# qkv channels of the first pass as seven products of halves, with the sums on VectorE, and reciprocals of softmax sums on 16 columns

## The chip, the core and the metric

The kernel runs on one core of one Trainium2 chip. The metric is the device time in microseconds of one execution; the kernel before takes 4035.16 us (median of 3 runs, 4035.09 to 4043.93).

## The reference

Two layers act on 8 images x of 256 channels and 64 x 64 pixels, all in fp32. The change touches two places: the division by the softmax sums in the first layer, and the product that makes the qkv channels in the second.

```python
# layer 0: attention of all pixels to 16 x 16 reduced ones
xr = norm(conv(x, w_sr, stride 4))
q, (k, v) = w_q @ x, split(w_kv @ xr)
out = softmax(q k^T * d**-0.5) v          # 8 heads of 32
x = x + gamma_s * (w_out @ out)
# layer 1: linear attention on qkv and on a convolved copy of it
qkv = w_qkv @ x                           # 768 channels from 256
agg = grouped_1x1(depthwise_5x5(qkv))
att = relu_linear_attention(concat(qkv, agg))
x = x + batch_norm(w_proj @ att)
```

## The kernel before

Three passes follow one another. `first_pass` (L575) does layer 0 and the qkv channels and leaves the results in HBM; `second_pass` (L961) does the convolution and the key-value sums; `third_pass` (L1281) applies them. The change lies in the first pass alone.

An image is kept in SBUF as two blocks of 128 channels by 4096 pixels, and cut into 8 strips of 512 pixels (QB). Two neighbouring strips make one class of pixels (`cls`). The 768 qkv channels are six blocks of 128: j = 0, 1 are q, 2, 3 are k, 4, 5 are v. Blocks of q and k go to HBM as planes with a zero border (`stage`), blocks of k and v also as transposed tokens (`turned`).

The loop over n (L905) walks through 256 steps: image b, strip s, channel half c, key half kc. A step issues, in this order: four score tiles of four heads on 32 rows each (`scores`, L758) and their exponentials on ScalarE (L764); the product with the values for the step before (`valued`, L775); in every second step the sums over keys (`counted`, L791), which use exponentials added up by GpSimd (`joined`, L786), then the division (`normed`), and the next queries (L743). What remains of a strip is spread over four further steps: in the first the output projection and its addition to x (`added`, L809 and L810), then three times two of its six qkv blocks (`qkv`, L834). In the last steps of an image TensorE also makes the reduced keys and values of the next one (`keys_values`, L671 to L734), with a norm on VectorE (L687 to L713). During the first image VectorE multiplies out the weights of the convolution as well (L647), one piece a step.

A qkv block is two matmuls of 128 x 128 by 512 into one PSUM bank, one for each half of the input channels. Score tiles, queries, outputs and qkv blocks all come from one set of five banks:

```python
def bank(name):
    return psum.tile([P, 512], F32, tag="mm", name=name, bufs=5)
```

`qkv` lets ScalarE copy the bank into `stage` (L843) and VectorE transpose it into `turned` (L853). `normed` copies the product with the values out of PSUM on ScalarE (L798), takes the reciprocal of 512 columns on VectorE (L799) and multiplies (L800). The sums are the same on all 32 rows of a head, since `ones_w` has 32 equal columns. Within an engine, instructions run in the order in which the program was built, where a scheduler has moved some of them a little.

Of the kernel before, what the change touches and what calls it, by code (L numbers as in the profile page):

```python
# [27 lines left out]
F32 = mybir.dt.float32  # L28
AF = mybir.ActivationFunctionType
ALU = mybir.AluOpType  # L30
AX = mybir.AxisListType

P = 128
# [4 lines left out]
NB = HH // R  # L38
# [3 lines left out]
D0 = C // HEADS  # L42
D1 = 8
NH = P // D1
KS = 5
QB = 512
NG = HW // QB
# [527 lines left out]
def first_pass(ctx: ExitStack, tc: tile.TileContext, a, fine, planes, x2d, kd, vd, wtd):  # L575
    nc = tc.nc
    B = a.x.shape[0]
# [5 lines left out]
    two = ctx.enter_context(tc.tile_pool(name="two", bufs=2))  # L583
    made = ctx.enter_context(tc.tile_pool(name="made", bufs=1))
    rest = ctx.enter_context(tc.tile_pool(name="rest", bufs=2))

    psum_early = ctx.enter_context(tc.tile_pool(name="psum_early", bufs=1, space=bass.MemoryType.PSUM))
    psum = ctx.enter_context(tc.tile_pool(name="psum", bufs=1, space=bass.MemoryType.PSUM))

    def bank(name):  # L590
        return psum.tile([P, 512], F32, tag="mm", name=name, bufs=5)

    def load(src, name):
        consts[name] = const.tile(list(src.shape), F32, tag=name, name=name)
        nc.sync.dma_start(consts[name], src)

    consts, x_tiles = {}, {}
# [11 lines left out]
    def load_consts():  # L609
        for n, src in (  # L610
            ("wq", a.w_q), ("wkv", a.w_kv), ("vec", a.vecs), ("gam", a.gamma_s), ("wout", a.w_out),
            ("wqkv", a.w_qkv), ("wsmall", a.w_small),
        ):
            load(src, n)

    ident = const.tile([P, P], F32, tag="ident", name="ident")
    make_identity(nc, ident)
# [122 lines left out]
    def queries(b, s, c):  # L740
        ps = bank(f"q_{b}_{s}_{c}")
        for ci in range(2):
            nc.tensor.matmul(  # L743
                ps,
                consts["wq"][:, ci, c * P : (c + 1) * P],
                x_tiles[b][:, ci, s * QB : (s + 1) * QB],
                start=(ci == 0),
                stop=(ci == 1),
            )
        qs = two.tile([P, QB], F32, tag="q", name=f"q_{b}_{s}_{c}")  # L750
        nc.scalar.copy(qs, ps)
        return qs
# [12 lines left out]
            es.append(e)  # L765
        return es

    sums, flats, stages = {}, {}, {}

    def valued(b, s, c, kc, es):  # L770
        if kc == 0:
# [16 lines left out]
    def counted(b, s, c, es):  # L788
        sums["den"] = psum_early.tile([P, QB], F32, tag="den", name=f"den_{b}_{s}_{c}")
        for h in range(4):  # L790
            nc.tensor.matmul(sums["den"][h * D0 : (h + 1) * D0], ones_w, es[h], start=True, stop=True)  # L791

    def normed(b, s, c):
        av, den = sums["av"], sums["den"]
        i = 2 * ((b * NG + s) * 2 + c)
        att = rest.tile([P, QB], F32, tag="att", name=f"att_{b}_{s}_{c}", bufs=4)
        r = rest.tile([P, QB], F32, tag="rden", name=f"rden_{b}_{s}_{c}")
        nc.scalar.copy(att, av)  # L798
        nc.vector.reciprocal(r, den)  # L799
        nc.vector.tensor_mul(att, att, r)  # L800
        nc.scalar.activation(den, den, AF.Copy, accum_out=seen[:, i : i + 1])
        nc.scalar.activation(den, r, AF.Copy, accum_out=seen[:, i + 1 : i + 2])
        return att

    def added(b, s, att, oc):
        xt, cols = x_tiles[b], slice(s * QB, (s + 1) * QB)
        ps = bank(f"o_{b}_{s}_{oc}")
        for c in range(2):
            nc.tensor.matmul(ps, consts["wout"][:, c, oc * P : (oc + 1) * P], att[c], start=(c == 0), stop=(c == 1))  # L809
        nc.vector.scalar_tensor_tensor(  # L810
            xt[:, oc, cols], ps, consts["gam"][:, 0:1], xt[:, oc, cols], ALU.mult, ALU.add
        )
        nc.sync.dma_start(x2d[b][oc * P : (oc + 1) * P, cols], xt[:, oc, cols])


    def new_stage(b, s):
        st = rest.tile([P, 4, 2, NB + 1, NB + 1], F32, tag="stage", name=f"stage_{b}_{s}")
        row, col = (0 if s // 4 else NB), (0 if s // 2 % 2 else NB)
        v = st.rearrange("p j f y x -> p (j f) y x")
        nc.gpsimd.memset(v[:, :, row], 0.0)  # L820
        nc.gpsimd.memset(v[:, :, :, col], 0.0)
        return st

    def interior(st, s):
        y, x = s // 4, s // 2 % 2
        return st[:, :, :, y : y + NB, x : x + NB]


    turned = {}

    def qkv(b, s, st, j):
        ps = bank(f"qkv_{b}_{s}_{j}")
        for ci in range(2):
            nc.tensor.matmul(  # L834
                ps,
                consts["wqkv"][:, ci, j * P : (j + 1) * P],
                x_tiles[b][:, ci, s * QB : (s + 1) * QB],
                start=(ci == 0),
                stop=(ci == 1),
            )  # L840
        cls, al = s // 2, s % 2
        if j < 4:
            nc.scalar.copy(interior(st, s)[:, j], ps.rearrange("p (f y x) -> p f y x", f=2, y=NB))  # L843
            nc.sync.dma_start(
                planes[b, j].rearrange("g (k i l f) e -> g k i l (f e)", k=4, i=D1, l=2)[:, cls, :, al],
                st[:, j].rearrange("p f y x -> p (f y x)"),
            )
        if j < 2:
            return
        if al == 0:  # L850
            turned[j] = rest.tile([P, NB // 2, 4, D0], F32, tag=f"turned{j}", name=f"turned_{b}_{s}_{j}", bufs=1)
        t = turned[j]
        nc.vector.transpose(  # L853
            t[:, :, 2 * al : 2 * al + 2].rearrange("p y f e -> p f y e"),
            ps.rearrange("p (f y e) -> p f y e", f=2, y=NB // 2),
        )
        if al == 1:
            for k in range(4):
                n, src = 4 * (j % 2) + k, t[k * D0 : (k + 1) * D0].rearrange("p y f e -> p y (f e)")
                if j < 4:  # L860
                    dst = kd[b][n].rearrange("a (y w) x b e -> a b (w x) y e", w=2)
                    nc.sync.dma_start(dst[cls // 2, cls % 2], src)
                else:
                    dst = vd[b][n][1 : NB2 + 1, 1 : NB2 + 1]
                    dst = dst.rearrange("(y w a) (x b) e -> a b w x y e", w=2, a=2, b=2)
                    for w in range(2):
                        nc.sync.dma_start(dst[cls // 2, cls % 2, w], src[w * NB : (w + 1) * NB])

# [9 lines left out]
    first = queries(0, 0, 0)  # L880
# [1 line left out]
        pass  # L882
    load_x(1)
    order = [(b, s, c, kc) for b in range(B) for s in range(NG) for c in range(2) for kc in range(2)]
    q, es, att, fill = {0: first}, {}, {}, []
    ahead = iter(())


    def after(b, s):
        def make_out(oc):  # L890
            return lambda: added(b, s, [att[b, s, 0], att[b, s, 1]], oc)

        def make_qkv(j):
            def go():
                if j == 2:
                    stages[b, s] = new_stage(b, s)
                qkv(b, s, stages[b, s], j)

            return go

        q = [make_qkv(j) for j in range(6)]
        return [[make_out(0), make_out(1)], [q[2], q[4]], [q[3], q[5]], [q[0], q[1]]]

    n_all = len(order)
    for n in range(n_all + 6):  # L905
        m = n - 1
        if n < n_all:
            b, s, c, kc = order[n]
            es[n] = scores(b, s, c, kc, q[n // 2])
        if 0 <= m < n_all:  # L910
            valued(*order[m], es[m])
            if order[m][3] == 1:
                counted(*order[m][:3], es.pop(m - 1))
                es.pop(m)
                att[order[m][:3]] = normed(*order[m][:3])
        if n < n_all and kc == 1:
            joined(es[n - 1], es[n])
        if n < n_all and kc == 0 and n + 2 < n_all:
            q.pop(n // 2 - 1, None)
            q[n // 2 + 1] = queries(*order[n + 2][:3])  # L920
        if n >= 6 and (n - 6) % 4 == 0 and (n - 6) // 4 < B * NG:
            fill += after((n - 6) // 4 // NG, (n - 6) // 4 % NG)
        next(weights, None)
        if n < n_all:
            b, at = n // 32, n % 32
            if at == 2:
                border(b)
            if b + 1 < B:
                if at == 10 and b > 0:
                    load_x(b + 1)  # L930
                if at == 12:
                    ahead = keys_values(b + 1)
                if 12 <= at < 20:
                    next(ahead)
                    next(ahead)
                elif at >= 20:
                    next(ahead, None)
        if fill:
            for f in fill.pop(0):
                f()  # L940
    for _ in weights:
        pass

# [685 lines left out]
```

## Time and profile before

| stretch | what runs | us |
|---|---|---|
| 0 to 53 | loads and the first reduced keys | 53 |
| 53 to 345 | first image (32 steps) | 293 |
| 345 to 2104 | images 2 to 8 | 1759 |
| 2104 to 2134 | rest of the last two strips | 30 |
| 2134 to 4032 | second and third pass | 1898 |

In the page each engine has its busy time and share of the span. A group of instructions has its line, engine and operation, the tiles it writes and reads, how many there are, busy time in us and the mean duration of one in ns, then the idle time of the engine before them and who ended it. In a timeline a row has the start, the duration, the engine, the line and, behind x, how many like instructions are merged in it; a matmul of fp32 makes two records. In the first pass one step takes 5.7 to 8.3 us where no reduced keys are made beside it.

### The profile page before, as it was taken

Reading aid. Unit: us, or ns where it says so; the run is one execution under the profiler, and the core shown is the slowest. Engines: PE = TensorE matmul, PEld = TensorE weight load, DVE = VectorE, ACT = ScalarE, POOL = GpSimd, SP = SyncE. Lnnn points to the kernel's source line nnn. Section 1 sums busy time; section 2 is a strip of 40 time slices with the busy share of each in tenths; the row PEclk is TensorE's granted clock in tenths of the full one; section 3 lists DMA queues with packets and bytes.
Section 4 is the critical chain, followed back from the end, with each engine's and each line's share of the span. In section 5 each row is a group of like instructions: output and inputs, shape, how many; then the busy total and the mean of one; then the engine's idle time right before and its main releaser. Section 6 shows DMA issues by size and latency. Waiting matters only on the chain. (4 is left out here: it accounts for less than half of the span.)

```text
span 4031.7 us, 69469 instructions
## 1 busy us (share of the span) xinstructions
PE 3967.1 (98%) x27266; PEld 2322.3 (58%) x27266; DVE 1943.0 (48%) x2724; ACT 1666.0 (41%) x3505; POOL 1207.0 (30%) x1234
## 2 busy tenths in 40 slices
PE   8999999999999999999999999999999998999998
PEld 4433433434334344343337888888888886565565
DVE  2554344343443434434444566666666664444443
ACT  2345455454554544545552222222222223454454
POOL 2333233332333333323333344444444440000000
PEclk9999999999999999999999999999999999999999
DMA  7655435344444344443539888778778756767674
GB/s 236 205 178 155 128 92 146 103 105 144 104 136 115 95 143 105 132 115 92 145 102 253 240 227 236 219 220 237 218 220 237 202 168 172 234 197 235 199 231 138
DMA packets 588321, 691.32 MB, mean 171 GB/s; under 512 B 62160, under 2 KB 431312, under 8 KB 583760
## 3 DMA queue, kind: packets, MB, share of 16 engines
q1 hardware_dynamic: 587984, 686.79, 59.7%
q8 instruction: 216, 3.54, 0.4%
q14 instruction: 121, 0.99, 0.1%
HBM read 412.54 MB, written 274.10 MB: 170 GB/s over the span
## 5 line engine op out<-in xcount | busy, mean ns | idle before, releaser
L786 POOL TENSOR_TENSOR e<-e,e 128x512 f32<-128x512 f32 x512 | 651.9, 1307 | 1204.1 <-PE av L775 1190.2
L799 DVE RECIPROCAL rden<-den 128x512 f32<-128x512 f32 x128 | 429.7, 3357 | 688.0 <-PE den L791 688.0
L764 ACT ACTIVATE e<-sc 128x512 f32<-128x512 f32 x1024 | 529.3, 602 | 419.2 <-PE sc L758 419.2
L834 PE MATMUL qkv<-x,wqkv 128*128 128x512 f32 x1536 | 701.1, 599 | 0.0
L834 PEld LDWEIGHTS qkv<-x,wqkv 128*128 128x128 f32 x1536 | 285.3, 190 | 372.7 <-issue 354.0
L1085 PE MATMUL cv<-w,c 128*128 128x128 f32 x3072 | 386.9, 280 | 4.9 <-POOL c L1029 4.9
L1085 PEld LDWEIGHTS cv<-w,c 128*128 128x128 f32 x3072 | 360.9, 193 | 33.5 <-issue 27.0
L853 DVE STREAM_TRANSPOSE turned<-qkv 128x512 f32<-128x512 f32 x256 | 177.3, 707 | 338.8 <-ACT stage L843 282.0
L758 PE MATMUL sc<-q,kk 32*128 32x512 f32 x2048 | 324.2, 640 | 11.0 <-DVE x L810 7.3
L1127 PE MATMUL sums<-vq,r 128*32 128x288 f32 x4096 | 303.1, 410 | 0.0
L1452 DVE TENSOR_TENSOR y<-z,xs 128x256 f32<-128x256 f32 x256 | 142.6, 644 | 315.9 <-ACT z L1443 290.9
L1101 ACT ACTIVATE r<-s 128x512 f32<-128x512 f32 x256 | 160.5, 627 | 299.9 <-DVE s L1100 299.5
L843 ACT COPY stage<-qkv 128x512 f32<-128x512 f32 x256 | 150.1, 586 | 304.3 <-PE qkv L834 294.6
L775 PE MATMUL av<-e,vv 128*32 128x512 f32 x2048 | 274.3, 608 | 0.0
L1443 ACT ACTIVATE z<-p,bn 128x256 f32<-128x256 f32 x256 | 133.7, 578 | 314.5 <-PE p L1434 240.6
L1089 PE MATMUL cv<-c,w 128*128 128x128 f32 x2048 | 256.4, 279 | 0.0
L743 PE MATMUL q<-x,wq 128*128 128x512 f32 x512 | 253.8, 618 | 0.0
L1434 PE MATMUL p<-att,wproj 128*128 128x512 f32 x512 | 249.4, 609 | 2.2 <-ACT att L1417 2.2
L1092 ACT COPY both<-cv 128x512 f32<-128x512 f32 x128 | 75.0, 586 | 421.8 <-PE cv L1085 364.8
L1434 PE MATMUL p<-agg,wproj 128*128 128x512 f32 x512 | 242.3, 596 | 0.0
L1089 PEld LDWEIGHTS cv<-c,w 128*128 128x128 f32 x2048 | 242.2, 194 | 0.0
L671 PE MATMUL sr<-x,wsr 128*128 128x256 f32 x1024 | 234.6, 385 | 7.1 <-DMA wsr<-in_w_sr_dram 7.1
(121 smaller groups left out, 5107.8 us busy)
## 6 DMA issues: line engine op xcount, KB each, us to landing
vq<-v SPq DMA_DIRECT2D x256, 384.0 KB
planes<-stage SPq DMA_DIRECT2D x256, 289.0 KB
d<-planes SPq DMA_DIRECT2D x128, 578.0 KB
raw<-planes SPq DMA_DIRECT2D x128, 272.0 KB
x<-in_xp_dram SPq DMA_DIRECT2D x64, 512.0 KB
wsr<-in_w_sr_dram SPq DMA_DIRECT2D x128, 256.0 KB
x<-x SPq DMA_DIRECT2D x128, 256.0 KB
k<-turned SPq DMA_DIRECT2D x256, 128.0 KB
```

What stands on the lines that cost most here:

```text
L671: nc.tensor.matmul(ps[:, oc], w[:, ci, oc * P : (oc + 1) * P], xt[:, ci, f * NK : (f + 1) * NK], start=(f == ci == oc == 0), stop=(f == R ...
L743: nc.tensor.matmul(ps, consts["wq"][:, ci, c * P : (c + 1) * P], x_tiles[b][:, ci, s * QB : (s + 1) * QB], start=(ci == 0), stop=(ci == 1),)
L758: nc.tensor.matmul(scs[h], kks[b][rows, c, kc * P : (kc + 1) * P], qs[rows], start=True, stop=True)
L764: nc.scalar.activation(e, scs[h], AF.Exp, scale=D0**-0.5)
L775: nc.tensor.matmul(sums["av"][cols], vvs[b][:, kc, c * P + h * D0 : c * P + (h + 1) * D0], es[h], start=(kc == 0), stop=(kc == 1),)
L786: nc.gpsimd.tensor_tensor(es0[h], es0[h], es1[h], ALU.add)
L799: nc.vector.reciprocal(r, den)
L834: nc.tensor.matmul(ps, consts["wqkv"][:, ci, j * P : (j + 1) * P], x_tiles[b][:, ci, s * QB : (s + 1) * QB], start=(ci == 0), stop=(ci == 1),)
L1085: nc.tensor.matmul(out, x, m, start=(da == 0), stop=(da == 1))
L1089: nc.tensor.matmul(out, m, x, start=(da == 0), stop=(da == 1))
L1127: nc.tensor.matmul(ps[h * D0 : (h + 1) * D0, : 36 * D1].rearrange("p (r n e) -> p r n e", r=3, e=D1), kt[:, par, h, 2 * r + c], vq[:, r : ...
L1434: nc.tensor.matmul(ps.rearrange("p (f q n) -> p f q n", f=4, q=4), wproj[:, j, oc * P : (oc + 1) * P], src, start=(j == 0), stop=(j == 3),)
```

## The change

The two blocks of a pair (q, k or v) and two strips are taken together: two halves of output channels, two halves of input channels, two strips. This is a product of 2 x 2 blocks, and it is made by seven products instead of eight. The combinations of weights are made once (`combine_weights`), the differences of x once for two strips (three on VectorE, one on GpSimd), and the products are summed as they leave PSUM: each of the seven is a matmul that fills a bank alone, p1 is copied by ScalarE, and VectorE adds the others to partial sums in SBUF. p5 is read twice. The q blocks are summed straight into `stage`; k and v blocks go through a tile `whole`, from which VectorE transposes and, for k, ScalarE copies. The work of two strips is laid over eight steps, with 4, 3, 4, 0, 3, 4, 3 products behind a step with outputs and differences.

In `normed` the sums are transposed in blocks of 32 x 32, the reciprocal is taken on 16 columns, and a second transpose spreads it again. The aim is one matmul in eight less on TensorE, and less work in the reciprocal.

```diff
+    halves = ctx.enter_context(tc.tile_pool(name="halves", bufs=1))
...
+        combine_weights()
...
+        nc.vector.tensor_add(s1, a21, a22)
+        nc.vector.tensor_sub(s2, s1, a11)
+        nc.vector.tensor_sub(s3, a11, a21)
+        nc.vector.tensor_sub(s4, a12, s2)
...
-        r = rest.tile([P, QB], F32, tag="rden", name=f"rden_{b}_{s}_{c}")
+        r = rest.tile([P, NB, D0], F32, tag="rden", name=f"rden_{b}_{s}_{c}", bufs=1)
+        one = two.tile([P, NB], F32, tag="one", name=f"one_{b}_{s}_{c}")
         nc.scalar.copy(att, av)
-        nc.vector.reciprocal(r, den)
+        nc.vector.transpose(r.rearrange("p n d -> p (n d)"), den)
+        nc.vector.reciprocal(one, r[:, :, 0])
+        r = rest.tile([P, NB, D0], F32, tag="rall", name=f"rall_{b}_{s}_{c}", bufs=1)
+        nc.vector.transpose(r, one.unsqueeze(2).to_broadcast([P, NB, D0]))
+        r = r.rearrange("p n d -> p (n d)")
         nc.vector.tensor_mul(att, att, r)
...
+    def differences(b, g):
...
+        nc.vector.tensor_sub(t1, b12, b11)
+        nc.vector.tensor_sub(t2, b22, t1)
+        nc.gpsimd.tensor_tensor(t3, b22, b12, ALU.subtract)
+        nc.vector.tensor_sub(t4, t2, b21)
...
-        for ci in range(2):
-            nc.tensor.matmul(
-                ps,
-                consts["wqkv"][:, ci, j * P : (j + 1) * P],
-                x_tiles[b][:, ci, s * QB : (s + 1) * QB],
-                start=(ci == 0),
-                stop=(ci == 1),
...
+        def product(i, w, x):
+            ps = bank(f"qkv_{name}_{i}")
+            nc.tensor.matmul(ps, w, x, start=True, stop=True)
+            return ps
...
+        def ended(r, h, u, ps, op=ALU.add):
...
+            if not turned:
+                nc.vector.tensor_tensor(inside, rows(u), rows(ps), op)
+                return
+            whole = part("whole", 2)
+            nc.vector.tensor_tensor(whole, u, ps, op)
+            if stages:
+                nc.scalar.copy(inside, rows(whole))
+            nc.vector.transpose(
+                turned[r][:, :, 2 * h : 2 * h + 2].rearrange("p y f e -> p f y e"),
+                whole.rearrange("p (f y e) -> p f y e", f=2, y=NB // 2),
             )
...
+        def p1():
+            ps = product(1, w[:, 0, 0], b11)
+            u[1] = part(1)
+            nc.scalar.copy(u[1], ps)
+
+        def p2():
+            ended(0, 0, u[1], product(2, w[:, 1, 0], b21))
+
+        def p6():
+            u[2] = part(2)
+            nc.vector.tensor_add(u[2], u[1], product(6, s2, t2))
+
+        def p7():
+            u[3] = part(3)
+            nc.vector.tensor_add(u[3], u[2], product(7, s3, t3))
+
+        def p4():
+            ended(1, 0, u[3], product(4, w[:, 1, 1], t4), ALU.subtract)
+
+        def p5():
+            ps = product(5, s1, t1)
+            ended(1, 1, u[3], ps)
+            u[4] = part(4)
+            nc.vector.tensor_add(u[4], u[2], ps)
+            stored(1)
+
+        def p3():
+            ended(0, 1, u[4], product(3, s4, b22))
+            stored(0)
...
+            work = [outputs(b, s) + [lambda b=b, s=s: differences(b, s // 2)]]
+            products = [p for pair in (1, 2, 0) for p in qkv_lazy(b, s // 2, pair)]
+            for i in (4, 3, 4, 0, 3, 4, 3):
+                work.append(products[:i])
+                products = products[i:]
```

In the changed kernel's lines the sum of p6 is L932, that of p7 L936, the second sum of p5 (u[4]) L945, and the sums of `ended` L888 and L891.

## The prediction

> **What bounds the kernel now.** I read the page's busy times first, then the busy times of stretches (the first pass ends at 2134 us), then the timelines of TensorE and VectorE for one strip, and last the places where TensorE waits. In the page, and in the stretch 1000 to 2000 us, TensorE is the engine that is never idle:
>
> ```profile
> PE 3967.1 (98%) x27266; PEld 2322.3 (58%) x27266; DVE 1943.0 (48%) x2724; ACT 1666.0 (41%) x3505; POOL 1207.0 (30%) x1234
> ...
> L799 DVE RECIPROCAL rden<-den 128x512 f32<-128x512 f32 x128 | 429.7, 3357 | 688.0 <-PE den L791 688.0
> ...
> L834 PE MATMUL qkv<-x,wqkv 128*128 128x512 f32 x1536 | 701.1, 599 | 0.0
> ```
> ```profile
> 1000.00:2000.00 1000.00, 1000.00 (x4320) 411.20 (x4319) 409.88 (x348) 492.55 (x1030) 334.89 (x319) 1.00 0.43 119
> ```
> The columns of the second view are the stretch, its length, then the busy us of PE, PEld, DVE, ACT and POOL. VectorE works 41% of it, so shortening the reciprocal (3.36 us) frees an engine that nobody waits for; what counts there is latency. A full busy figure doesn't say that TensorE never waits, because overlapping matmul records cover gaps. The timeline shows that (start, us, what):
>
> ```profile
> 1908.13 1.14 PE L758 MATMUL sc<-q,kk 32*128 32x512 f32 x8
> 1909.20 1.07 PE L775 MATMUL av<-e,vv 128*32 128x512 f32 x8
> 1910.19 3.70 PE L834 MATMUL qkv<-x,wqkv 128*128 128x512 f32 x8
> 1913.83 1.14 PE L758 MATMUL sc<-q,kk 32*128 32x512 f32 x8
> ...
> 1918.57 3.60 PE L834 MATMUL qkv<-x,wqkv 128*128 128x512 f32 x8
> 1922.10 1.41 PE L758 MATMUL sc<-q,kk 32*128 32x512 f32 x8
> 1923.44 1.07 PE L775 MATMUL av<-e,vv 128*32 128x512 f32 x8
> ...
> 1928.06 1.14 PE L758 MATMUL sc<-q,kk 32*128 32x512 f32 x8
> ```
> A record lasts 599 ns but the next begins before it ends, so the spacing counts. Eight qkv records take 3.53 us (1918.57 to 1922.10): 8 x 0.43, and 0.09 for going over to the small score tiles. After an av group the first record costs 0.11 more (1910.19 to 1913.83). The steps of one strip last 8.27, 5.70, 8.27 and 5.97 us, from one score group to the next: 28.21 a strip, 56.42 for two. The 5.97 holds a wait of 0.27: the group at 1922.10 takes 1.34 until av where it takes 1.07 elsewhere. The next view shows what such a wait is:
>
> ```profile
> 1046.03 2.73 DVE L713 TENSOR_SCALAR xr<-xr,vec 128x256 f32<-128x256 f32 x2
> ...
> 1048.69 1.30 DVE L853 STREAM_TRANSPOSE turned<-qkv 128x512 f32<-128x512 f32 x2
> 1048.69 1.87 PE L758 MATMUL sc<-q,kk 32*128 32x512 f32 x8
> ...
> 1050.49 1.07 PE L775 MATMUL av<-e,vv 128*32 128x512 f32 x8
> ```
> Four score tiles and the qkv tiles share five PSUM banks. The fourth score tile takes a bank that VectorE has yet to read; VectorE was held by the norm, and the score group grew from 1.07 to 1.80 us. TensorE lost those 0.73 us for good.
>
> **What the Trainium skill says.** "TensorE: Matmul & The Clock Gate", Step-by-step: only weight loads are pulled ahead, matmuls stay in program order; so a score tile that waits holds all behind it, as the last view shows. "PSUM — Partial Sum Buffer", The four PSUM rules: a matmul output is at most one bank of 512 fp32; each product is thus a bank of its own, against two matmuls to a bank before. "SBUF — State Buffer", Who interferes with whom: a VectorE operation with both inputs in SBUF shuts out GpSimd's reads and is shut out by them, for whole instructions. The trace agrees: the square of xr (L689) took 1.29 us at 1030.84 beside GpSimd's additions and 0.69 at 41.32 without them.
>
> **The change, part by part.** *Removed on TensorE:* 96 groups (8 images, 4 pairs of strips, 3 pairs of channel blocks) go from eight matmuls to seven: 96 matmuls of two records, 192 x 0.43 = 82 us. In the built order two strips are again eight steps: outputs; 4 products; 3; 4; outputs; 3; 4; 3. Without waits they last 8.27 + 5.70 + 7.41 + 5.70 + 8.27 + 4.84 + 8.27 + 4.84 = 53.30 us, so 3.12 less than before (2.58 of work, 0.54 of old waits).
>
> *Added on VectorE:* seven sums a group instead of copies on ScalarE. For their durations the trace has three neighbours of the same form (a sum with one PSUM input, a transpose of its result, another such sum):
>
> ```profile
> 2301.11 0.69 DVE L1206 TENSOR_TENSOR tok<-ng,den 128x512 f32<-128x512 f32 x1
> 2301.84 0.71 DVE L1213 STREAM_TRANSPOSE att<-tok 128x512 f32<-128x512 f32 x1
> 2302.47 0.65 DVE L1100 TENSOR_TENSOR s<-cv,both 128x512 f32<-128x512 f32 x1
> ```
> So 0.73 from a sum to the transpose that needs it, 0.64 on to the next, 0.65 for a sum that follows another. VectorE starts 0.63 after the last record of a bank starts (1913.83 - 0.52 = 1913.31, to the transpose at 1913.93 in VectorE's timeline), and TensorE 0.05 after VectorE ends (in the view before, the first transpose ends at 1048.69 + 0.70 = 1049.39, and the fourth score tile starts 1.05 ahead of av, at 1049.44). By sums, two strips cost VectorE 21 x 0.65 + 8 x 0.7 + 3 differences of 0.7, against 4 x (3.36 - 0.71 - 0.25 - 0.71) saved on reciprocals (0.25 is interpolated between 3.36 for 512 columns and 0.55 for 64): about 9 us more in 57, under 60% busy. Throughput is no limit.
>
> *The new wait:* in the built program the fourth score tile after a step of products takes the bank of p6 (steps of 4) or p5 (steps of 3), in 172 of 192 steps. p5's bank is free only after both of its sums. With t = 0 at the first record of the step:
> - Step of 3, k channels: p4's sum starts at 0.43 + 0.63 = 1.06, its transpose 1.79, p5's first sum 2.43, u4 3.07, over at 3.72, TensorE 3.77. It would have come at 6 x 0.43 + 0.11 = 2.69. Wait 1.08.
> - The same for v channels, after av: all 0.11 later, wait 1.08.
> - Step of 3, q channels (no transposes): p5's first sum 1.39 + 0.63 = 2.02, u4 2.67, over 3.32, TensorE 3.37 against 2.80: 0.57.
> - Step of 4, k and v: p2's sum 2.02, transpose 2.75, p6's sum 3.39, over 4.04, TensorE 4.09 against 3.65: 0.44 each. For q, none: p6's sum is over at 3.47, as TensorE comes at 3.55.
>
> The sum is 1.08 + 1.08 + 0.57 + 0.44 + 0.44 = 3.61 for two strips. Behind a waiting score tile stand its av, den and all later matmuls, and no other engine's slack gives that back. Two strips: 53.30 + 3.61 - 56.42 = +0.5 us; times 31 (the last pair is the tail), +15.
>
> *Smaller terms (my estimates):* the differences contend with GpSimd (0.69 to 1.29, with the p2 sum behind them): 0.2 x 31 = 6. In the first image 32 multiplications for the weights (L647, 1952 ns mean) stand in VectorE's queue, some between p2's sum and its transpose or between p4 and p5; some five delay TensorE by about 2 us, 0 to 30 for the range: +10. In 7 steps with the norm the fourth score tile waits for the first one's exponential, about 1.8, where before it was 0.73: +2. Tail: 21 products of 0.86 = 18 us run beside 29 VectorE operations of 0.64 = 18.6, so a start and an end show: +1. The combinations of weights stand ahead of the first norm (first VectorE work at 40.53) and wait for wqkv, issued at 32.0: 0 to 3, taken as 1. Fewer and larger stores, fewer stage copies and the shorter reciprocal cost nothing on the path: their queues have idle time. Tiles of the later passes keep their addresses.
>
> Sum: 15 + 6 + 10 + 2 + 1 + 1 = +35, so 4035 + 35 = 4070.
>
> **Rivals.** (1) *The waits are hidden*, if the bank is free in time: then 3.12 x 32 = 100 us go, about 3940, or part of it. For it: VectorE has idle time over all. Against it: the wait is latency from p4 to u4, in an order that idle time can't change. 0.16. (2) *Break-even*: the waits sum to 3.1 instead of 3.6 and the first image costs little: within 12 us of 4035. 0.17. (3) *Longer chains*: a sum of the form takes 0.75, as the scalar_tensor_tensor at L810 does, which adds 0.3 to each of four chains (1.2 x 31 = +37), and the weights' multiplications cost 30 instead of 10: 4127 or more. 0.10. (GpSimd sets a floor under rival 1: its four additions, 4.94 us from 2.26 us after an odd score group at 1908.13, gate den 7.2 us after that group; a step of 3 comes there at 4.84 + 1.94 = 6.8, so some 0.4 would be lost in any case, twice a pair.)
>
> **How the numbers follow.** The forecast above has 0.57: 4047 to about 4120. Slower 0.57 + 0.10, within 0.3% 0.17, faster 0.16. The range 4012 to 4120 leaves out most of rival 1 and the far half of rival 3, 2 in 10.
>
> **What would show it.** Right: the score groups after products take about 2.1 us in steps of 3 and 1.5 in steps of 4, waiting for the sums of L932 and L945; two strips last near 57 us; qkv matmuls 1344 records. Wrong: score groups back at 1.07 and two strips at 53 to 54 us (rival 1); sums above 0.7 us (rival 3); or den waiting for GpSimd in place of the banks.

## The result and the profile after

The changed kernel takes 4055.15 us (median; 4052.98 to 4062.72), beside it the kernel before took 4034.73: ratio 1.0051, 95% interval 1.0038 to 1.0064. The change makes the kernel 20 us slower.

The page's first line and the stretch of 1000 to 2000 us of the kernel after (columns as before: stretch, length, busy us of PE, PEld, DVE, ACT, POOL, clock, DMA share, GB/s):

```profile
PE 3982.1 (98%) x27074; PEld 2318.8 (57%) x27074; DVE 2262.4 (56%) x3752; ACT 1644.2 (41%) x3473; POOL 1275.1 (31%) x1394
```
```profile
1000.00:2000.00 1000.00, 995.73 (x4166) 405.10 (x4165) 555.56 (x836) 475.99 (x998) 363.60 (x390) 1.00 0.45 117
```

192 matmul records are gone, and TensorE's busy time has still grown, from 3967.1 to 3982.1 us. VectorE works 56% of the stretch instead of 41%, so it isn't full. TensorE's timeline of a step of four products, one of three and their score groups shows where the matmul time went:

```profile
1922.34 1.88 PE L875 MATMUL qkv<-differences,combined 128*128 128x512 f32 x4
1924.14 1.64 PE L774 MATMUL sc<-q,kk 32*128 32x512 f32 x8
1925.72 1.06 PE L791 MATMUL av<-e,vv 128*32 128x512 f32 x8
...
1931.11 1.02 PE L875 MATMUL qkv<-x,combined 128*128 128x512 f32 x2
1932.06 2.17 PE L774 MATMUL sc<-q,kk 32*128 32x512 f32 x8
1934.16 1.07 PE L791 MATMUL av<-e,vv 128*32 128x512 f32 x8
```

A score group took 1.07 us until av. It takes 1.58 here after four products (1924.14 to 1925.72) and 2.10 after three (1932.06 to 1934.16): waits of 0.5 and 1.03. They count as busy, because the records on both sides of a wait overlap; that is how "busy" grew while work went. What the fourth score tile of the group at 1932.06 waits for is in VectorE's timeline:

```profile
1930.45 0.69 DVE L891 TENSOR_TENSOR part_whole<-part,qkv 128x512 f32<-128x512 f32 x1
1931.17 0.71 DVE L894 STREAM_TRANSPOSE turned<-part_whole 128x512 f32<-128x512 f32 x1
1931.81 0.65 DVE L891 TENSOR_TENSOR part_whole<-part,qkv 128x512 f32<-128x512 f32 x1
1932.38 0.68 DVE L945 TENSOR_TENSOR part<-part,qkv 128x512 f32<-128x512 f32 x1
```

These are p4's sum, its transpose, and both sums of p5, the last over at 1932.38 + 0.68 = 1933.06. Then p5's bank is free, and the fourth score tile starts 1.05 ahead of av, at 1934.16 - 1.05 = 1933.11. It is no single case: in images 2 to 8 the fourth score tile waits for VectorE and starts 1.05 us after the first in 49 groups, 0.52 in 48 and 0.59 in 28.

The eight steps of two plain strips (strips beside which no reduced keys are made; the other pairs are called pairs with keys) now last 8.77, 4.84, 9.30, 4.84, 8.84, 5.70, 7.92 and 6.73 us: 56.94, against 56.42 before. From the starts of the score groups, the first pass adds up so:

| stretch | before | after | difference |
|---|---|---|---|
| first image (32 steps) | 276.7 | 264.1 | -12.6 |
| images 2 to 7 | 1555.9 | 1578.9 | +23.0 |
| last image, to its last score group | 218.2 | 221.2 | +3.0 |
| from there to the end of the first pass | 29.5 | 38.1 | +8.6 |

With a start 0.5 earlier that is +21.4 (from unrounded times); the later passes add 1.3, together the 22.7 us between the two profiled spans. The products come later in the order than before, so part of the first image's gain is only work moved to the end.

### The profile page after: what moved, and what is told of

It reads as the page before. It is cut to its first block, busy times and chain, and to the rows that moved or that the text cites. A ratio compares the mean times of both kernels' runs of the same rounds, so it can differ in the third digit from the quotient of the medians.

```text
span 4054.4 us, 70276 instructions
## 1 busy us (share of the span) xinstructions
PE 3982.1 (98%) x27074; PEld 2318.8 (57%) x27074; DVE 2262.4 (56%) x3752; ACT 1644.2 (41%) x3473; POOL 1275.1 (31%) x1394
## 3 DMA queue, kind: packets, MB, share of 16 engines
q14 instruction: 131, 1.07, 0.1%
## 5 line engine op out<-in xcount | busy, mean ns | idle before, releaser
L774 PE MATMUL sc<-q,kk 32*128 32x512 f32 x2048 | 418.2, 641 | 7.5 <-ACT e L780 3.6
L891 DVE TENSOR_TENSOR part_whole<-part,qkv 128x512 f32<-128x512 f32 x256 | 170.7, 670 | 219.6 <-PE qkv L875 215.8
L774 PEld LDWEIGHTS sc<-q,kk 32*128 32x128 f32 x2048 | 130.0, 183 | 276.3 <-issue 138.3
L875 PE MATMUL qkv<-differences,combined 128*128 128x512 f32 x576 | 278.7, 593 | 0.8 <-DVE differences L848 0.8
L687 PEld LDWEIGHTS sr<-x,wsr 128*128 128x128 f32 x1024 | 193.3, 192 | 76.3 <-issue 32.8
L831 PE MATMUL o<-att,wout 128*128 128x512 f32 x512 | 231.9, 594 | 0.0
```

What stands on the lines that cost most here:

```text
L687: nc.tensor.matmul(ps[:, oc], w[:, ci, oc * P : (oc + 1) * P], xt[:, ci, f * NK : (f + 1) * NK], start=(f == ci == oc == 0), stop=(f == R ...
L774: nc.tensor.matmul(scs[h], kks[b][rows, c, kc * P : (kc + 1) * P], qs[rows], start=True, stop=True)
L875: nc.tensor.matmul(ps, w, x, start=True, stop=True)
```

## The experiments

Theory: what the seven products save, the score tiles lose waiting for banks that VectorE gives back late. It is the latency of a chain that counts, not VectorE's load. Rivals: VectorE's load; the reciprocals; the weights' multiplications in the first image. Two strips and steps below are read from the starts of the score groups, as above.

**The reciprocals alone.**

```diff
 # before.py, normed
...
-        nc.vector.reciprocal(r, den)
+        nc.vector.transpose(r.rearrange("p n d -> p (n d)"), den)
+        nc.vector.reciprocal(one, r[:, :, 0])
+        r = rest.tile([P, NB, D0], F32, tag="rall", name=f"rall_{b}_{s}_{c}", bufs=1)
+        nc.vector.transpose(r, one.unsqueeze(2).to_broadcast([P, NB, D0]))
+        r = r.rearrange("p n d -> p (n d)")
```

> The kernel before with the new reciprocal alone (two turns and 16 columns), nothing else changed. Theory (bank latency: what the change loses, it loses in the score tiles that wait for sums): VectorE is not what a plain step waits for, so no change beyond the 0.73 us score-tile waits in steps with the norm, at most some -5 us: 4028 to 4037, two plain strips 56.4 us as before. Rival (the reciprocals are part of what moved the time): 10 us or more away from 4035, to either side.

4018.47 us, ratio to before 0.9947 (0.9934 to 0.9961): 18 us faster, and two strips 55.88. My expectation was wrong: the waits of 0.27 us in the kernel before, two in two strips, came from the reciprocal. The way from one to the other leads through ScalarE. In the kernel before, ahead of the score group at 1922.10, VectorE's lines and then ScalarE's:

```profile
1916.96 3.36 DVE L799 RECIPROCAL rden<-den 128x512 f32<-128x512 f32 x1 [2.31 <-PE den L791]
...
1921.61 1.31 DVE L853 STREAM_TRANSPOSE turned<-qkv 128x512 f32<-128x512 f32 x2 [0.49 <-ACT stage L843]
```
```profile
1920.42 0.58 ACT L801 ACTIVATE den<-den 128x512 f32<-128x512 f32 x1 [1.06 <-DVE rden L799]
...
1921.00 0.58 ACT L843 COPY stage<-qkv 128x512 f32<-128x512 f32 x1
```

The reciprocal reads den until 1920.32. ScalarE's sum over den (L801) writes den in place and waits for that; the copy of the qkv bank into `stage` stands behind this sum, and the transpose that frees the bank starts when the copy is over. VectorE itself stood idle for 0.49 us before the transpose. TensorE's timeline of the kernel with the new reciprocals, at the group that took 1.34 until av before:

```profile
1902.93 3.60 PE L840 MATMUL qkv<-x,wqkv 128*128 128x512 f32 x8
1906.46 1.14 PE L758 MATMUL sc<-q,kk 32*128 32x512 f32 x8
1907.53 1.07 PE L775 MATMUL av<-e,vv 128*32 128x512 f32 x8
```

1.07 again. In images 2 to 8 the kernel before has 37 waits of 0.27 us, 10 us in all, and this one has none. Of the rest, 4 us are in the first image, where the steps can't be matched one by one. So of the two parts of the change one gains 18 us, and the products, beside it, lose 4055.15 - 4018.47 = 37.

**More work inside the chain, and the same work behind it.**

```diff
 # extra_inside: after.py, p5
             nc.vector.tensor_add(u[4], u[2], ps)
+            nc.vector.tensor_add(u[4], u[2], ps)
             stored(1)
 # extra_last: after.py, p3
-            ended(0, 1, u[4], product(3, s4, b22))
+            ps = product(3, s4, b22)
+            ended(0, 1, u[4], ps)
+            nc.vector.tensor_add(u[4], u[2], ps)
```

> The kernel after with p5's second sum (u4) computed twice, one after the other: 96 more sums on VectorE, in the chain between p5 and the release of its bank. Theory (bank latency): each adds its 0.65 us to the wait of the fourth score tile after a step of three products: 3 x 0.65 = 1.95 us in two strips, 31 x 1.95 = 60 us in all: 4115. Rival (VectorE's load counts, not the place in the chain): 96 x 0.65 = 62 us of work on an engine that is busy 56% moves the time by the same small amount here and in the run with the extra sum at the end.

> The kernel after with an extra sum of the same form (u2 plus the product p3, written where u4 was, which nothing reads any more) behind p3's own sum and its transpose: 96 more sums on VectorE, behind the chain. Theory (bank latency): nobody waits for the end of that queue in plain steps, so 4055 to 4061, with a few us for the tail, where VectorE's sums set the pace. Rival (VectorE's load): the same as with the extra sum inside.

Inside: 4132.54 us, 77 more than after (ratio to before 1.0245, 1.0227 to 1.0263). Behind: 4057.19 (1.0050, 1.0034 to 1.0065), 2 more. The same 96 sums cost 77 us in the chain and next to nothing behind it, so the place counts and the load does not. After q's three products the trace names the extra sum (L946) as what TensorE waits for (TensorE's timeline; the second row is the two records of the fourth score tile):

```profile
1976.01 1.13 PE L774 MATMUL sc<-q,kk 32*128 32x512 f32 x6
1977.32 1.12 PE L774 MATMUL sc<-q,kk 32*128 32x512 f32 x2 [0.18 <-DVE part L946]
1978.37 1.07 PE L791 MATMUL av<-e,vv 128*32 128x512 f32 x8
```

After the three products of k and v the fourth score tile waits longer too, but for something else: it starts 1.81 to 1.87 us after the first, and the trace puts that down to the exponential of the first score tile. It starts while VectorE still reads p5's bank (1962.92 against 1963.30 in one case), so it has taken another bank. There the extra sum lengthens the wait by this way round, and not by its own 0.65 us. The three steps with such a wait are longer by 0.76, 0.72 and 0.82 us, 2.30 in two strips, where I expected 1.95. Images 2 to 8 are 71 us longer together; in this is one step an image that is 1.6 us longer still, where the granted clock falls to 0.50 for 3.4 us.

**Without most of the weights' multiplications**, in both kernels.

```diff
 # conv_weights
             for i in range(8):
-                w = made.tile([P, 2, 6 * 16, D1], F32, tag="wb", name=f"wb_{j}_{i}", bufs=1)
                 gs = slice(2 * i, 2 * i + 2)
-                nc.vector.tensor_tensor(
...
+                if i == 0:
+                    w = made.tile([P, 2, 6 * 16, D1], F32, tag="wb", name=f"wb_{j}_{i}", bufs=1)
+                    nc.vector.tensor_tensor(
...
                 nc.sync.dma_start(wtd[j][:, gs], w.rearrange("p g n o -> p g (n o)"))
```

> The kernel after without 28 of the 32 multiplications of the convolution weights on VectorE in the first image (1952 ns each): only the first of each eight is computed, and is stored eight times, so the weights of the second pass are partly left out. Theory (these stand in VectorE's queue inside the chains that TensorE waits for): 10 to 16 us less than 4055, and the kernel before loses 0 to 5 by the same edit. Rival (the first image loses to transfers or to the keys' chain): within 4 us of 4055.

> The kernel before with the same edit: 28 of the 32 multiplications of the weights are left out, and the first of each eight is stored eight times. Theory: before the change the banks of products were mostly read by ScalarE, so VectorE's queue holds up little: 0 to 5 us less than 4035. Rival: the same gain as in the changed kernel, so that the multiplications are no part of the difference.

After: 4036.35 us, ratio to the kernel before 0.9995 (0.9987 to 1.0004), against 1.0051 with them: 19 to 23 us. Before: 3999.90 us, 0.9907 (0.9893 to 0.9920): 37 us. The multiplications cost both kernels, and the kernel before some 15 us more; I had it the other way round. Of the 15 the first pass shows 8: without the multiplications it is 30.1 us longer after the change than before, from the first score group to its end, and with them 21.9. The rest lies in its start and in the later passes, and can't be put down to the edit with certainty. The view of the multiplications' line says why they cost more than their 1.76 us (the median of one). First the kernel before, then the kernel after (us, times):

```profile
its engine sat idle before it (us, times) until:
  DMA wt<-wb: 58.9, 18
```
```profile
its engine sat idle before it (us, times) until:
  DMA wt<-wb: 36.1, 12
```

There is one buffer for the products of the weights. A multiplication at the head of VectorE's queue waits for the store of the last one, and everything behind it waits too, the readers of banks among them. In the changed kernel VectorE stood 23 us less like that. Why its multiplications fell in better places I didn't try.

**The transposes behind the sums.**

```diff
 # after.py, ended()
-            nc.vector.transpose(
+            late.append(lambda: nc.vector.transpose(
...
 # p7 behind u[3], p5 behind u[4], p3 behind its sum
+            turn()
 # defer_turns
+        def turn():
+            while late:
+                late.pop(0)()
 # late_turns, in turn()
-                late.pop(0)()
+                tc.keep_in_program_order(late.pop(0)())
```

> The kernel after with only the order on VectorE changed inside a group of products: the transpose of p2's sum is issued after p7's sum, that of p4's after both sums of p5. Theory (bank latency): the transposes (0.73 + 0.64 - 0.65 = 0.7 us each) leave the chain that the fourth score tile waits for. Steps of three products for k and v then wait as those for q do, 0.57 instead of 1.03; steps of four wait 0 instead of 0.5. That is 1.9 us in two strips: 55.0 instead of 56.94, and 31 x 1.9 = 59 us in all: 3996. Rival (VectorE's load, or its contention with GpSimd): the same instructions, 4055 within 5.

4074.05 us, 1.0091 (1.0076 to 1.0107). In plain strips this run is no test of the theory. VectorE's built order had stayed as it was there, and two strips last 56.94 as in the kernel after: the order of the lines isn't the order of issue. But in some steps of the first image, and in one step of each of images 2 to 7, the one behind the norm of the reduced keys, the transposes did move behind p5's second sum. VectorE's lines there in the third image:

```profile
789.67 1.27 DVE L891 TENSOR_TENSOR part_whole<-part,qkv 128x512 f32<-128x512 f32 x2
790.87 0.67 DVE L950 TENSOR_TENSOR part<-part,qkv 128x512 f32<-128x512 f32 x1
791.46 1.29 DVE L894 STREAM_TRANSPOSE turned<-part_whole 128x512 f32<-128x512 f32 x2
```

The kernel after has the two transposes ahead of that sum. The fourth score tile of this step now starts 2.74 us after the first instead of 1.81, and in three of the six images the granted clock then falls to 0.50 for 3.4 us: the step takes 12.72 or 14.4 us instead of 11.79. That makes 10.6 of the 10.7 us by which images 2 to 7 are longer. Differences of that size say little on any cause without the steps of the trace. With the order pinned everywhere:

> What defer_turns was meant to be: there the order in the built program had stayed as it was, because the scheduler and not the order of the lines places VectorE's instructions. Here each transpose is pinned behind the sums, so that VectorE's built order is p2, u2, u3, transpose; p4, p5, u4, transpose, transpose; p3, transpose. Theory (bank latency): the fourth score tile waits 0.57 instead of 1.03 us after steps of three products for k and v, and 0 instead of 0.5 after steps of four: two plain strips 55.0 instead of 56.94, in all about 31 x 1.9 = 59 us less than 4055: 3996. Rival (VectorE's load, the same instructions): 4055 within 5.

4086.29 us, 1.0129 (1.0112 to 1.0146), slower still, and yet the waits that were named went. The steps that held 1.03 are 9.30 to 8.84 and 6.73 to 6.27 us, the group after four products is back at 1.07 until av, and the one after three takes 1.64 instead of 2.10 (TensorE's timeline, the same two steps as in the first of the kernel after):

```profile
1940.31 1.88 PE L875 MATMUL qkv<-differences,combined 128*128 128x512 f32 x4
1942.12 1.14 PE L774 MATMUL sc<-q,kk 32*128 32x512 f32 x8
1943.19 1.07 PE L791 MATMUL av<-e,vv 128*32 128x512 f32 x8
...
1950.02 1.71 PE L774 MATMUL sc<-q,kk 32*128 32x512 f32 x8
1951.66 1.07 PE L791 MATMUL av<-e,vv 128*32 128x512 f32 x8
```

1.92 us went from two strips (0.46 and 0.5, twice each), as forecast. But two strips last 58.5: den now waits 0.5 in one step and 2.96 in another. For what, GpSimd's timeline shows:

```profile
1897.40 0.16 POOL L855 MEMSET stage<- 128x68 f32 x1 [11.38 <-DMA planes<-stage]
1897.61 0.22 POOL L856 MEMSET stage<- 128x68 f32 x1
1897.72 4.96 POOL L802 TENSOR_TENSOR e<-e,e 128x512 f32<-128x512 f32 x4
```

The zeroing of a stage stands ahead of den's additions and waits until the stage's store is over. Moved away and pinned:

```diff
 # differences(): the k stages are made here, behind t3, and no longer in qkv()
+        early[b, g] = [new_stage(b, g, j) for j in (2, 3)]
 # new_stage(), this line and the next alike
-        nc.gpsimd.memset(st[:, :, 0 if g // 2 else NB], 0.0)
+        tc.keep_in_program_order(nc.gpsimd.memset(st[:, :, 0 if g // 2 else NB], 0.0))
```

> late_turns (transposes pinned behind the sums) with one thing more: the zeroing of the two k stages on GpSimd is issued behind the differences, a step ahead of their products, and the zeroing of all stages is pinned to its place in the order. In late_turns the scheduler had put it ahead of the additions for den while the stage's store still ran, so GpSimd stood until the store was over and den waited up to 2.4 us once in two strips. Theory (bank latency, with GpSimd's held queue as the wait that took its place in late_turns): score tiles wait as in late_turns (0.57 us after steps of three, 0 after steps of four) and den no longer waits: two plain strips 55.0 us (53.30 + 3 x 0.57), 31 x 1.9 = 59 us less than 4055: 3996, and so below the kernel before. Rival 1 (the additions on GpSimd themselves are too late, whatever stands ahead of them): two strips 56 us or more, 4025 or more. Rival 2 (VectorE's load): 4055 or more.

4038.42 us, ratio to before 1.0004 (0.9995 to 1.0012), 17 less than after, where 59 were expected. Two strips: 8.84, 4.84, 8.84, 5.70, 8.12, 6.27, 8.27, 4.84, which makes 55.72. That is 53.30 + 3 x 0.57 + 0.70; the last term is a den group that still waits for the additions, which start behind the differences and the zeroing. 31 x 1.22 = 38 us should have come. The rest went in the last pair of strips of images 2 to 7, which takes 63.0 to 64.6 us where the kernel after takes 61.2, and behind the last score group (41.5 instead of 38.1). In those pairs it is again the step behind the norm, which takes 14.4 or 16.0 us instead of 11.79. In late_turns, with the same order of sums and transposes, it takes 12.72 at full clock; the rest, 15 us in the six images, comes with the clock. Stretches of this kernel in the third image, then of the kernel after (the clock is the third figure from the end):

```profile
780.00:785.00 5.00, 4.98 (x18) 1.09 (x18) 2.46 (x4) 1.76 (x3) 0.01 (x1) 0.50 0.45 67
785.00:790.00 5.00, 5.00 (x17) 2.90 (x14) 2.37 (x4) 2.32 (x7) 0.00 (x0) 0.82 0.89 140
```
```profile
785.00:790.00 5.00, 5.00 (x27) 2.46 (x26) 4.56 (x8) 2.86 (x8) 0.00 (x0) 1.00 0.58 88
```

The granted clock falls to half for some microseconds, once in each of these images, in or just behind a score group that waits for its banks. Without these 15 us the run would take about 4023, an estimate from this one profiled execution: ahead of the kernel before, behind the reciprocals alone.

**The products ahead of av and den**, to put other matmuls between the last product and the next score tiles.

```diff
 # one step n of the loop, in words
-scores; av, den, division of n-1; additions; q; products
+scores; products; av, den, division of n-1; additions; q          # order_first (after), before_order
+scores; q; products; av, den, division of n-1; additions          # order_mid (after), recip_mid
```

> The kernel after with one thing moved: in each step the products (and the outputs) stand ahead of av, den and q on TensorE instead of behind them, so that 1 to 3.8 us of other matmuls lie between the last product and the next score tiles. Theory (bank latency): the waits of about 0.5, 1.03, 0.5, 1.03 and 0.57 us, 3.6 in two strips, go to about 0; two plain strips 53.3 to 53.8 us instead of 56.94, and 31 x 3.2 to 3.6 us less in all: 3943 to 3960. Rival 1 (VectorE and GpSimd have more work and that sets the pace): the instructions are the same, so 4050 or more. Rival 2 (a new wait takes the place of the old one: a product now takes the bank of a score tile whose exponential has to be over first, or den waits for the additions on GpSimd): two strips 55 us or more, 4000 or more.

> The kernel before with the same move of its products ahead of av, den and q. Theory (bank latency): it takes away only the two waits of 0.27 us in two strips: 31 x 0.54 = 17 us less, 4018. If the move itself were worth what it is worth in the changed kernel (rival: the move helps for another reason than the banks of the products), some 90 us less: 3940.

order_first: 4041.13 us, 1.0014 (1.0005 to 1.0022), two strips 57.0; what it gains on the kernel after lies in the first image (5 us) and in pairs with keys (9). before_order: 4053.54, 1.0043 (1.0030 to 1.0057), two strips 56.82 instead of 56.42. Neither came to what I expected. In order_first a product waits for the bank of q, and q's copy on ScalarE stands behind the sum over den, which waits for VectorE to have read den. TensorE's line, then ScalarE's two:

```profile
1906.66 2.27 PE L875 MATMUL qkv<-x,wqkv 128*128 128x512 f32 x4 [1.08 <-ACT q L767]
```
```profile
1905.45 0.58 ACT L823 ACTIVATE den<-den 128x512 f32<-128x512 f32 x1 [3.05 <-DVE rden L817]
...
1906.03 0.58 ACT L767 COPY q<-q 128x512 f32<-128x512 f32 x1
```

In before_order no such wait shows. A step there takes 8.47 us where it took 8.27. TensorE goes from small to full tiles and back once more in it (scores, products, av instead of scores, av, products), and the two changes cost about 0.1 us each: behind score tiles the eight records take 3.63 us until the next group, behind q 3.53, and q takes 1.91 ahead of score tiles, 1.82 ahead of the products. So I put q ahead of the products, which takes away the wait for q; and for comparison the same order in the kernel before with the new reciprocals:

> The kernel after with TensorE's order in each step changed to score tiles, q, products (or outputs), av, den. Against order_first, q stands ahead of the products, so the first product no longer takes the bank of a q whose copy on ScalarE is still to come. Theory (bank latency, with q's copy as the new wait in order_first): no wait on either side; two plain strips 53.3 to 53.8 us instead of 56.94: 31 x 3.1 to 3.6, so 3943 to 3960. Rival (another new wait: products wait for the exponentials of the score tiles whose banks they take, or den for GpSimd): two strips 55 us or more, 4000 or more.

> The kernel before with the new reciprocal and the same order in each step (score tiles, q, products, av, den), so that only the products differ from order_mid: eight matmuls and copies instead of seven and sums. Theory: recip_only had no waits left in plain strips (55.88 us for two), so the order gives nothing here: 4018 within 6, and order_mid is faster than it by the 82 us of matmuls or a little less. Rival (the order itself is what helps): under 4000 here.

order_mid: 4058.25 us, 1.0054 (1.0041 to 1.0068), two strips 57.6. Now the products take banks of score tiles whose exponentials are late, because the same sums over den and its reciprocal stand between them on ScalarE:

```profile
1919.91 2.32 PE L875 MATMUL qkv<-differences,combined 128*128 128x512 f32 x4 [0.30 <-ACT e L780]
```

Score tiles wait as well: in 38 groups of images 2 to 8 the fourth starts some 0.9 us late. recip_mid: 4041.46 us, 1.0015 (1.0008 to 1.0022), where 4018 within 6 was expected. Two strips last 55.88 as in the run with the reciprocals alone, but two of the pairs with keys take 1.3 and 1.8 us and the first image 10 us longer. So the order costs 23 us by itself, and even at the same order the seven products are 17 us slower than the eight. No run with seven products beats the kernel before; the reciprocals alone (4018.47 us) do.

## Why the prediction was right

The forecast was slower, 4070, likeliest by the bank waits; measured 4055. The main term was right in size and mechanism; of the smaller ones some were wrong, and one wait was not in it. Point by point:

- *The new wait, +15:* right. Forecast for two strips 56.91, measured 56.94; single waits of 1.03, 1.03, 0.57, 0.5 and 0.5 against 1.08, 1.08, 0.57, 0.44 and 0.44, whose errors of 0.05 cancel. 31 x 0.52 = 16 us, if every pair pays what a plain one does. The runs with an extra sum inside and behind show that it is latency, and the pinned transposes took off just the part that the transposes have in it.
- *Throughput is no limit:* right (2 us for 96 sums behind the chain). The sum for VectorE, as it is written, gives 14.6 us and not 9, but its eight transposes stand in the kernel before as well; without them it is 9, and measured are 146 us more in 1000, or 8 in 57.
- *The 0.54 us of old waits:* the size was right, the owner wasn't. I counted it among what the new steps save, and said that the shorter reciprocals free an engine that nobody waits for; recip_only shows that it is they that take these waits off, by way of ScalarE's queue. Against the reciprocals alone the products take two strips from 55.88 to 56.94. By the traces images 2 to 7 are 32.6 us longer for them (24 x 1.06 = 25 of it at the rate of plain pairs), the last image 5.1 and the tail 9.1 longer, the first image 8.5 shorter.
- *Contention of the differences, +6:* mis-sized; in plain pairs it is 0. What "SBUF — State Buffer", Who interferes with whom, in the Trainium skill, says is borne out: the last difference (L850) took 1.65 us at 1920.07, while GpSimd made its own difference (L849, 1919.39 to 1921.18), and the one ahead of it, which had started before GpSimd's, 0.69. But nobody waits for it: the step after it has its products behind a score group and av.
- *Norm steps, +2:* right. In all seven the fourth score tile waits for the first one's exponential and starts 1.81 us after the first, as forecast; the pair of strips with such a step costs 0.31 more than a plain pair, 1.9 in images 2 to 7.
- *Not in the forecast:* images 2 to 7 cost 23.0 us, 10.5 more than 24 plain pairs. Besides the norm, TensorE waits once in each of them for weights of the reduced keys that come by DMA:

```profile
PE sr L687 <- DMA wsr<-in_w_sr_dram: 4.2, 6, 1.6
```

  (counted idle us, times, longest.) The step that holds this wait takes 13.0 to 14.2 us, where 11.73 before and a bank wait of 0.57 make 12.3: 5.7 us in the six. The kernel before has no such wait in these images; why the weights come later now was not tried. Two pairs an image also had one old wait to lose, and not two: 3.2 us. So the terms for contention and norm, 8 together, come near the 10.5 only by luck.
- *Weights in the first image, +10:* the wrong sign. They cost the kernel before 37 us and the kernel after 19 to 23, so the change gains 8 there by the traces of the first pass (15 by the times). I priced the multiplications by their own time and not by the wait for their one buffer at the head of the queue.
- *Tail and start, +2:* in the two runs without the weights the first image and the tail together differ by 2.7 us, of which 4 x 0.52 = 2.1 are bank waits. About right.

The forecast was 15 us too slow: 18 by the sign of the weights, and about 3 back by the pairs with keys. Its range, 4012 to 4120, was wide enough for both. Of the rivals, the hidden waits fell with the first score group of the trace; the longer chains too (0.65 to 0.69 us a sum). The floor by GpSimd noted under rival 1 is real: with the bank waits shortened, den waited for the additions at once (0.5 and 0.70 us, without the held store).

What stays open is whether seven products can pay at all here. Each wait that was taken away uncovered another on TensorE's in-order queue: GpSimd's additions, q's copy, the exponentials. The sums over den on ScalarE, which hold q's copy and the exponentials and which held the copies into `stage` in the kernel before, were not moved.

## What to carry to other kernels

Count matmuls last: first follow each PSUM bank from the matmul that fills it, through the in-order queues of its readers, to the next matmul that takes it, and multiply that latency by how often it comes. A change of two parts is split before it is judged; here one part gained 18 us and the other lost 37. And read the order that was built, not the order of the lines: an edit meant for every group moved the transposes in one step an image, and that made up more than half of 0.5%.

## What was not expected of the hardware

The granted clock fell to half for 3.4 to 6.8 us at a time, at waits of TensorE of which the trace counts well under a microsecond as idle. In late_early the score group at 777.25 us takes 4.77 us until av instead of 1.07, and the trace counts 0.45 of it as idle:

```profile
778.82 3.26 PE L774 MATMUL sc<-q,kk 32*128 32x512 f32 x4 [0.45 <-DVE part_whole L892]
782.02 1.94 PE L791 MATMUL av<-e,vv 128*32 128x512 f32 x8
```

The av group takes 1.71 us until den where it takes 0.88. The clock falls at 780.02, as the fourth score tile starts, 2.77 us after the first; records cover waits, as above, so the real idle time in these 2.77 us is longer than what is counted. "TensorE: Matmul & The Clock Gate", HAM oscillation — how this bites in real kernels, in the Trainium skill, gives the abstract rule as no idle gaps above about 3.4 us; the next section there, A second HAM failure mode: psum-queue depth-cycling, tells of a kernel whose clock swings because short idles between groups come often enough. These traces fit the second better, for no gap near 3.4 us was there, though here it is one wait and not a row of them. And a wait of this kind isn't enough. The kernel after waits at the same place (2.86 us until av, 0.42 counted as idle) and keeps full clock in all images. So does late_turns, with 3.79 until av and the fourth tile 2.74 us after the first, hardly shorter than in late_early, where the clock fell in all six images; in defer_turns, with the same 3.79, it fell in three of six. What tips it isn't settled. In the third image the step takes 16.02 us against 12.72 in late_turns, so the clock cost 3.3 us, more than six of the waits of 0.5 us that the run had taken away.

Going over between full and small tiles costs TensorE about 0.1 us each time, as the 0.09 and 0.11 of the prediction have it. What wasn't expected is that a change of order adds such changes, and has to earn them back first (before_order: 8.47 us for a step of 8.27).
